# Ternary weights asked for one chunk ahead, a written order for VectorE, and feed-forward's first input between the last unit's projections

## The chip, the cores and the metric

The kernel runs on one core of one Trainium2 chip. A core has a matrix engine (TensorE, PE in the profile; PEld are its weight loads), VectorE (DVE), ScalarE (ACT), GpSimd (POOL) and SyncE (SP), which here only issues DMAs. Each engine carries out its own instructions in the order in which they stand in its queue, and waits on semaphores for the others. The metric is the device time of one execution in microseconds; lower is better.

## What is computed

The input is x, 2 sequences of 1024 rows of 512. Four residual layers follow one another:

```python
x = x + attn_a(layernorm(x))      # gated linear recurrence
x = x + ffn(layernorm(x))         # ternary feed-forward
x = x + attn_b(layernorm(x))      # differential attention
x = x + ffn(layernorm(x))         # the same feed-forward again
```

The change lies in the first layer and in the entry to the second. The first is, with 16 heads of 32:

```python
q, k, v, a, g = split(x @ w_in.T, 5)
q = q * rsqrt(mean(q*q, per head) + eps);  k = tanh(k)
a = clip(sigmoid(a + 2), 0.6, 0.9995);     u = k * v
# per chunk of 64 rows, the state being carried from chunk to chunk
prefix = cumprod(a);  acc = cumsum(u / max(prefix, 1e-6))
mem = prefix * (state + acc)
y = sigmoid(g) * (q * mem) + (1 - sigmoid(g)) * v
return y @ w_out.T
```

The feed-forward takes its weights in ternary form. In groups of 64, `scale = max(mean(|w|), 1e-8)`, and the weight becomes `clip(round(w/scale), -1, 1) * scale`. It computes `silu(x @ gate.T) * (x @ up.T)`, scales it by its root mean square, and multiplies it by the projection.

## The kernel before

All 16 tiles of x (128 rows each) stay in SBUF as `xres`. The first layer, called the gated stage here, works on four blocks t = 0 to 3 of 512 rows. What happens in a block:

- **Input.** `Input(t)` takes the layernorm statistics of the block's four tiles (`layernorm_stats`: two VectorE operations a tile, lines 109 and 110, a square root on ACT, line 112, a reciprocal, line 116). `normal(j)` normalises tile j on VectorE (line 127), and `turn(j)` transposes it on TensorE (line 136) and copies it on ACT (line 265) into `xt`.
- **Queries.** `queries(t, xt)` projects q in four pieces (`pq`), copies and squares each on ACT, and sums the squares by head with matmuls into `pss` (line 280). A square root on ACT and three VectorE operations (lines 300 to 304, among them a reciprocal of 3.3 us) make `rq`, the heads' factors.
- **Units.** For each quarter c of the channels, TensorE makes k and v (`kv`), then a and g (`ag`), each projection with `project` (8 matmul records). Then a small matmul `pr` (line 389) spreads `rq`. ACT makes u = tanh(k), v, a and the gate. VectorE clips a, makes `prefix` with a scan, runs the state's scan `mem`, multiplies it by `qn` and by the gate. GpSimd makes the products u·v and u·prefix, mem − v and the sum `yt`; in the very last unit VectorE does these too (`other`).
- **Output.** The products of `yt` with `w_out` (line 421), tile by tile, are added to `xres` on VectorE (line 426). The next block's queries stand before the output products of a block.

PSUM has two double banks ("big") for `kv` and `ag` and four single ones ("bank") for all else.

Beside this runs the making of ternary weights, in 16 chunks f of 768 KB. `Ternary.__init__` issues three loads on SyncE's queue (line 155), then ACT takes magnitude (line 157) and sign (line 159). `mean(i)` is a matmul `pm` on TensorE (line 166) and a copy on ACT (line 167), three a chunk. `finish` is six VectorE operations (lines 171 to 179). `quantise(i)` does piece i of the chunk at hand: 0 to 2 are means, and 3 is `finish`, the write of the result to DRAM as `w_kept` (line 319), and the next chunk's `Ternary`. The pool that holds the chunks has two buffers of each kind, except `one`. Blocks 0 to 2 each work on four chunks: in the units, one ends at c = 1 and one at c = 3; one has its means in the queries and ends after them; and one has its pieces behind the output products of tiles 0 to 3. In block 3 each of c = 0 to 2 has a chunk of its own. Chunk 0 is done in block 0's queries.

The order of instructions is settled in two ways. Inside `tc.manual_schedule` an engine's instructions keep the order of the program text. Other engines are ordered by a planner, which places what it expects to be ready. In the gated stage, TensorE has the written order (up to the last block's output products), and VectorE has it in the very first input alone.

The feed-forward (`feed_forward`, also for the last layer) begins by asking for all 16 chunks of `w_kept` (line 569). Its first input is `FeedForwardInput(which, 0, ...)`: statistics of x tiles 0 to 3, which are final once block 0's output is added, four normalised tiles, four transposes, and for each a rounded copy `hi` on ACT (line 474) and the difference `lo` on VectorE (line 475). They stand ahead of its first gate projection, `g` (line 524).

Of the kernel before, what the change touches and what calls it, by code (L numbers as in the profile page):

```python
# [10 lines left out]
F32 = mybir.dt.float32  # L11
F32R = mybir.dt.float32r
# [5 lines left out]
P = 128  # L18
D = 512
# [4 lines left out]
BLK = 512  # L24
# [18 lines left out]
def kernel(  # L43
# [95 lines left out]


# [3 lines left out]
    class Ternary:  # L144
# [3 lines left out]
        def __init__(self, pool, f, tiles):  # L148
            self.pool, self.f, self.n = pool, f, f"{f}_{tiles[0]}"
            self.shape = [P, len(tiles), D]  # L150
            self.w = pool.tile(self.shape, F32R, tag="w32", name=f"w32_{self.n}")
            w32 = self.w.bitcast(F32)
            for i, e in enumerate(tiles):
                src = w_pt[ts(f, P), :] if e == 2 else w_gu[e * NF + f].rearrange("p c n -> p (c n)")
                nc.sync.dma_start(out=w32[:, i, :], in_=src)
            self.mag = pool.tile(self.shape, BF, tag="mag", name=f"mag{self.n}")
            nc.scalar.activation(self.mag, w32, AF.Abs)
            self.sign = pool.tile(self.shape, BF, tag="sign", name=f"sign{self.n}")
            nc.scalar.sign(self.sign, w32)
            self.scale = None  # L160

# [20 lines left out]
    with ExitStack() as s:  # L182
# [15 lines left out]
        w_q, w_k, w_v = (load_w_in(i) for i in range(3))  # L198
# [6 lines left out]
        chunk = [Ternary(tp, 0, range(3))]  # L205
        w_a, w_g = (load_w_in(i) for i in (3, 4))
        load_x(TPB, 2 * TPB)
        w_out = wa.tile([P, NKC, D], F32, name="w_out")
# [64 lines left out]
        def queries(t, xt):  # L273

            q = ap_.tile([P, NKC, BLK], F32, tag="q", name=f"q{t}")
# [21 lines left out]
            mean_square(*late.pop())  # L297
            rq = ap_.tile([16, BLK], F32, tag="rq", name=f"rq{t}")
            nc.scalar.activation(rq, pss[:16, :], AF.Sqrt, bias=rms_eps[:16])
            nc.vector.reciprocal(rq, rq)  # L300
            parts = rq_parts[t % 2]
            hi, lo = parts[:16], parts[32:48]
            nc.vector.tensor_copy(hi, rq)
            nc.vector.tensor_sub(lo, rq, hi.bitcast(F32))
            quantise(3)
            return q, parts

        load_x(2 * TPB, NTT)

        def quantise(i):  # L310

            now = chunk[0]
            if now is None:
                return
            if i < 3:
                now.mean(i, bank)
                return
            now.finish(now.w)
            nc.sync.dma_start(out=w_kept[now.f].bitcast(F32), in_=now.w.bitcast(F32))
            chunk[0] = Ternary(tp, now.f + 1, range(3)) if now.f + 1 < NF else None  # L320

        order = ExitStack()
        order.enter_context(tc.manual_schedule(engines={mybir.EngineType.PE}))
        before = [None] * NKC
        first = Input(0, at_once=False)
        with tc.manual_schedule(engines={mybir.EngineType.DVE}):
            for j in range(TPB + 1):
                if j < TPB:
                    first.measure(j)
                if j:  # L330
                    first.normal(j - 1)
                    first.turn(j - 1)
        xt = first.xt
        q, rq = queries(0, xt)
        for t in range(NBLK):
            yt = wa.tile([P, NKC, BLK], F32, tag="yt", name=f"yt{t}")
            following = None
            for c in range(NKC):
                n = f"{t}_{c}"
                kv, ag = big(f"kv{n}"), big(f"ag{n}")  # L340
                project(kv[:, 0, :], w_k, c, xt)
                project(kv[:, 1, :], w_v, c, xt)

                if t < NBLK - 1:
                    pieces = ((2,), (), (3,)) if c % 2 else ((0,), (1,), ())
                else:
                    pieces = ((0, 1), (2,), (3,)) if c < NKC - 1 else ((), (), ())
                for i in pieces[0]:
                    quantise(i)
                project(ag[:, 0, :], w_a, c, xt)  # L350
                project(ag[:, 1, :], w_g, c, xt)
                for i in pieces[1]:
                    quantise(i)
                if following and c > 1:
                    for j in (2 * c - 4, 2 * c - 3):
                        following.turn(j)
# [9 lines left out]
                other = nc.gpsimd if (t, c) < (NBLK - 1, NKC - 1) else nc.vector  # L366
# [12 lines left out]


# [6 lines left out]

                pr = bank(f"pr{n}")
                nc.tensor.matmul(pr, headrow[:, c, :], rq, start=True, stop=True)
                qn = ap_.tile([P, BLK], F32, tag="qn", name=f"qn{n}")  # L390
                nc.vector.tensor_mul(qn, pr, q[:, c, :])
                nc.vector.tensor_mul(mem, mem, qn)
                other.tensor_sub(mem, mem, v)
                nc.vector.tensor_mul(mem, mem, gate)
                other.tensor_add(yt[:, c, :], mem, v)

                if t + 1 == NBLK and c == 0:
                    ff_stats = layernorm_stats(range(TPB), "f0_0")
                if t + 1 < NBLK and c < 2:
                    if c == 0:  # L400
                        following = Input(t + 1)
                    following.normal(0 if c == 0 else 1)
                for i in pieces[2]:
                    quantise(i)
                if following and c == 2:
                    following.normal(2)
                    following.normal(3)

            if following:
                xt = following.xt  # L410
                q_next, rq_next = queries(t + 1, xt)
            products = [(j, k) for j in range(TPB) for k in range(NKC)]
            if not following:

                order.close()
                products.sort(key=lambda jk: jk[1] == NKC - 1)
            po = {}
            for j, k in products:
# [5 lines left out]
                if k == NKC - 1:  # L424
                    xi = xres[t * TPB + j]
                    nc.vector.tensor_add(xi, xi, po[j])
                    if following:
                        quantise(j)
            if following:
                q, rq = q_next, rq_next  # L430

    edge_sb = ctx.enter_context(tc.tile_pool(name="edge", bufs=1, reuse_waits="tile"))
# [20 lines left out]
    class FeedForwardInput:  # L455


        def __init__(self, which, t, pool, tag, stats=None):
            self.n = f"{which}_{t}"
            self.which, self.tiles = which, range(t * TPB, (t + 1) * TPB)  # L460
            self.stats = stats or layernorm_stats(self.tiles, f"f{self.n}")
            self.xs = pool.tile([P, 2, NKC, BLK], F32R, tag=tag, name=f"xs{self.n}", bufs=1)
            self.xn = {}

        def normal(self, j):
            i = self.tiles[j]
            self.xn[j] = normal(i, j, self.stats, f"f{self.which}_{i}")

        def tile(self, j, psum):
            if j not in self.xn:  # L470
                self.normal(j)
            pt = transposed(self.xn.pop(j), f"f{self.which}_{self.tiles[j]}", psum)
            hi, lo = (self.xs[:, e, :, ts(j, P)] for e in range(2))
            nc.scalar.copy(hi, pt)  # L474
            nc.vector.tensor_sub(lo, pt, hi.bitcast(F32))

# [5 lines left out]
    def feed_forward(which, store, first=None, beside=None):  # L482


        with ExitStack() as s:
# [84 lines left out]
            if not first:  # L570
                first = FeedForwardInput(which, 0, edge_sb, "xt", ff_stats)
                for j in range(TPB):
                    first.tile(j, ring)
# [44 lines left out]
        0, False, None,  # L618
# [533 lines left out]
```

## Time and profile before

| | us |
|---|---|
| median of 3 runs | 2145.2 (2144.91 to 2147.58) |
| the profiled execution | 2146.65 |
| its span, first to last instruction | 2144.9 |
| TensorE busy | 2108.8 |
| VectorE busy | 1069.1 |
| ScalarE busy | 835.2 |
| GpSimd busy | 449.8 |

The gated stage and the entry to the feed-forward fill the first 400 us of the span. All rows are of one execution. In a timeline, a row has its start, the time of its group from first start to last end, engine, line, operation, output and inputs and how many instructions are merged; brackets give the idle time of the engine before the row and who ended it. In a list of waits the figures are the total, the number of waits and the longest.

### The profile page before, as it was taken

To read this page: it belongs to the slowest core of one execution; us is meant where nothing else is said; L and a number is where in the kernel's file an instruction comes from. 1 tells how busy PE (TensorE), PEld (TensorE's weight loads), DVE (VectorE), ACT (ScalarE), POOL (GpSimd) and SP (SyncE) were. 2 spreads that over 40 slices of the span, in tenths; PEclk is the share of its full clock that TensorE was granted. 3 is DMA by queue.
4 is the path that set the end of the run, shared out by engine and by line. 5 is a ranking of instruction groups with operands and counts; after the bars stand their busy time and mean duration, and the time that the engine had idled before them with its cause. 6 is when DMAs were issued, how large, how long until landed. Compare 5 with 4: busy or idle time off the path is not lost.

```text
span 2144.9 us, 28054 instructions
## 1 busy us (share of the span) xinstructions
PE 2108.8 (98%) x10615; PEld 1242.2 (58%) x10624; DVE 1069.1 (50%) x2272; ACT 835.2 (39%) x1590; POOL 449.8 (21%) x812
## 2 busy tenths in 40 slices
PE   8999999999999999999999999999999999999998
PEld 3444444688888854444444444444545447888887
DVE  5766686533343234555555465464546662433322
ACT  4444333234344322444444422243434523333333
POOL 1312212122122221111111113021212221121212
PEclk9999999999999999999999999999999999999999
DMA  6111211600000111111110101201110033000000
GB/s 255 59 59 62 86 59 74 250 1 1 1 1 1 35 46 37 41 26 41 23 44 21 46 8 37 57 20 42 24 32 15 14 111 132 20 1 20 1 20 20
DMA packets 50999, 98.71 MB, mean 46 GB/s; under 512 B 10800, under 2 KB 19120, under 8 KB 50864
## 3 DMA queue, kind: packets, MB, share of 16 engines
q1 hardware_dynamic: 50864, 96.93, 13.8%
q8 instruction: 83, 1.36, 0.3%
q14 instruction: 52, 0.43, 0.1%
HBM read 58.75 MB, written 16.78 MB: 35 GB/s over the span
## 4 chain that ended last, share of the span: by engine, by line
PE 83%; DVE 8%; DMA 4%; ACT 2%; issue 1%; POOL 1%; SPq 1%; DVEq 0%; ACTq 0%; POOLq 0%
PE y L904 12%; PE g L524 11%; PE u L524 11%; PE f_out L545 11%; PE s L805 10%; PE pq L737 8%; PE t L866 8%; PE pv L702 3%; PE b_out L965 2%; DMA w<-in_w_pt_dram 1%; DMA w_kept<-w 1%; DVE one L174 1%; PE kv L269 1%; DVE w L179 1%; PE ag L269 1%
## 5 line engine op out<-in xcount | busy, mean ns | idle before, releaser
L882 ACT ACTIVATE pr<-t 128x512 f32<-128x512 f32 (+3 forms) x768 | 314.8, 497 | 380.6 <-PE t L874 380.4
L815 DVE CUSTOM_DVE_ANT_0 s<-s,causal 128x128 f32<-128x128 f32 (+3 forms) x512 | 245.3, 510 | 126.1 <-PE s L805 117.4
L904 PE MATMUL y<-pr,val 128*64 128x512 f32 (+3 forms) x1536 | 291.6, 501 | 0.2 <-POOL pr L885 0.2
L539 POOL TENSOR_TENSOR ssq<-ssq,sq 128x512 f32<-128x512 f32 x120 | 155.9, 1299 | 603.6 <-ACT sq L538 603.6
L530 DVE TENSOR_TENSOR h<-h,u 128x512 f32<-128x512 f32 x128 | 88.0, 688 | 362.0 <-PE u L524 355.9
L524 PE MATMUL g<-xs,w 128*128 128x512 f32 x1024 | 262.4, 398 | 0.9 <-ACT xs L474 0.7
L545 PE MATMUL f_out<-w,hs 128*128 128x512 f32 x1024 | 257.7, 394 | 0.3 <-DVE hs L533 0.3
L820 DVE TENSOR_REDUCE nmax<-s 128x1 f32<-128x512 f32 x256 | 165.0, 686 | 184.4 <-PE s L805 184.3
L524 PE MATMUL u<-xs,w 128*128 128x512 f32 x1024 | 256.4, 392 | 0.0
L805 PE MATMUL s<-gr,gr 32*128 32x512 f32 (+3 forms) x1536 | 248.8, 492 | 2.6 <-DVE nmax L815 2.6
L524 PEld LDWEIGHTS u<-xs,w 128*128 128x128 f32 x1024 | 192.4, 188 | 43.5
L545 PEld LDWEIGHTS f_out<-w,hs 128*128 128x128 f32 x1024 | 191.6, 188 | 43.9 <-DVE hs L533 1.1
L524 PEld LDWEIGHTS g<-xs,w 128*128 128x128 f32 x1024 | 190.9, 189 | 44.0 <-ACT xs L474 0.9
L866 PE MATMUL t<-gr,gr 32*128 32x512 f32 (+3 forms) x1536 | 198.8, 533 | 0.0
L904 PEld LDWEIGHTS y<-pr,val 128*64 128x64 f32 x1536 | 93.5, 136 | 179.9 <-issue 105.7
L737 PE MATMUL pq<-b_xt,w_qk 128*128 128x512 f32 x384 | 176.0, 603 | 0.0
L805 PEld LDWEIGHTS s<-gr,gr 32*128 32x128 f32 x1536 | 147.6, 185 | 46.8 <-issue 14.0
L532 ACT CAST hs<-h 128x512 fp32r<-128x512 f32 x128 | 79.4, 621 | 236.6 <-DVE h L530 236.6
L885 POOL TENSOR_SCALAR_AFFINE_SELECT pr<-pr 128x256 f32<-128x256 f32 x256 | 101.3, 408 | 332.2 <-ACT pr L882 332.2
L529 ACT ACTIVATE h<-g 128x512 f32<-128x512 f32 x128 | 76.5, 598 | 224.3 <-PE g L524 224.1
L533 DVE TENSOR_TENSOR hs<-h,hs 128x512 fp32r<-128x512 f32 x128 | 88.6, 692 | 83.1 <-ACT hs L532 83.1
L737 PEld LDWEIGHTS pq<-b_xt,w_qk 128*128 128x128 f32 x384 | 69.6, 189 | 88.0 <-issue 74.0
(155 smaller groups left out, 2211.0 us busy)
## 6 DMA issues: line engine op xcount, KB each, us to landing
w<-w_kept SPq DMA_DIRECT2D x32, 768.0 KB, 8.7
w_kept<-w SPq DMA_DIRECT2D x16, 768.0 KB, 3.2
gr<-gr SPq DMA_DIRECT2D x96, 128.0 KB, 2.3
w<-in_w_gu_dram SPq DMA_DIRECT2D x32, 256.0 KB, 2.8
share<-ys SPq DMA_DIRECT2D x128, 64.0 KB, 2.0
w_in<-in_w_in_t_dram SPq DMA_DIRECT2D x5, 1024.0 KB, 11.2
x<-in_x_dram SPq DMA_DIRECT2D x16, 256.0 KB, 7.1
w<-in_w_pt_dram SPq DMA_DIRECT2D x16, 256.0 KB, 3.5
```

The source lines that it names most:

```text
L524: nc.tensor.matmul(po, ws[f][:, part, ts(k, P)], xs[:, e, k, :], start=(k == 0 and e == 0), stop=(k == NKC - 1 and e == 1),)
L533: nc.vector.tensor_sub(hp[:, 1, :], h, hp[:, 0, :].bitcast(F32))
L539: nc.gpsimd.tensor_add(ssq, ssq, sq)
L545: nc.tensor.matmul(po[j], hp[:, e, ts(j, P)], ws[f][:, 2, :], start=(f == 0 and e == 0), stop=(f == NF - 1 and e == 1),)
L737: nc.tensor.matmul(po, w[:, k, ts(kind, P)], xts[b][:, k, ts(e, BLK)], start=(k == 0), stop=(k == NKC - 1),)
L805: nc.tensor.matmul(part, queries[:, ts(j, P)], keys[:, first : first + nk], start=True, stop=True,)
L815: nc.vector.tensor_tensor_reduce(part, part, causal[:, BLK - part.shape[-1] :], -1.0, 3.0e38, ALU.add, ALU.min, top,)
L820: nc.vector.tensor_reduce(top, part, AX.X, ALU.max, negate=True)
L866: nc.tensor.matmul(banks[u, e][:, :nq], keys[:, ts(kb, P)], queries[:, (qb + 1) * BLK - nq : (qb + 1) * BLK], start=True, stop=False,)
L882: nc.scalar.activation(pr[:, e, :nq], banks[u, e][:, :nq], AF.Exp)
L885: nc.gpsimd.affine_select(out=pr[:, :, :P], in_=pr[:, :, :P], compare_op=ALU.is_ge, fill=0.0, base=0, pattern=[[0, 2], [1, P]], channel_mu ...
L904: nc.tensor.matmul(y[64 * e : 64 * e + 64, lo:], all_values[:, HV * (NH * kb + h) : HV * (NH * kb + h) + 64], pr[:, e, : BLK - lo], start= ...
```

## The change

1. **Chunks.** `Ternary.__init__` now only issues the loads. ACT's magnitude and sign are in a new method `begin`. Two chunks are in hand: the one worked on and the one already asked for. `finish` of chunk f is followed by `begin` of f + 1 and the loads of f + 2. Chunk 1's loads stand before those of `w_out`; x tiles 8 to 15 are loaded after block 0's queries in the text.
2. **Order.** VectorE has the written order in the whole gated stage, and both engines keep it to the end of the last block's output products. Within a unit, `pr` and `qn` stand ahead of the state's scan. A block's `Input` with its statistics is moved forward: `Input(1)` stands behind block 0's queries, and `Input(t + 2)` at the end of block t. `normal(0)` and `normal(1)` stand in units 0 and 1 behind `qn`; the transposes stand between the k/v and the a/g projections of units 2 and 3, with `normal(2)` and `normal(3)` between those of unit 2.
3. **Queries.** The last `pss` matmul with the square root (`roots`) and the three VectorE operations (`factors`) are moved: in block 0 behind the first k projection, otherwise behind the output products of tile 0, with the chunk's `finish` between them. The next chunk's pieces are spread anew over the output products.
4. **Feed-forward's first input** is made in the last block: statistics and `normal(0)`, `normal(1)` in unit 2 behind the product with `qn`, the four tiles before and after the a projection of unit 3. Its `xs` takes the tile in which `w_q` and `w_k` now lie together. The last block's output products run over k = 0 and 1 of all tiles first, then k = 2, then k = 3.

The core of the diff:

```diff
+        def begin(self):
+            pool, w32 = self.pool, self.w.bitcast(F32)
             self.mag = pool.tile(self.shape, BF, tag="mag", name=f"mag{self.n}")
             nc.scalar.activation(self.mag, w32, AF.Abs)
             self.sign = pool.tile(self.shape, BF, tag="sign", name=f"sign{self.n}")
             nc.scalar.sign(self.sign, w32)
             self.scale = None
+            return self
...
-        w_q, w_k, w_v = (load_w_in(i) for i in range(3))
+        w_qk = edge_sb.tile([P, 2, NKC, D], F32, tag="xt", name="w_in_qk")
+        w_q, w_k = w_qk[:, 0], w_qk[:, 1]
...
-        chunk = [Ternary(tp, 0, range(3))]
+        chunk = [Ternary(tp, 0, range(3)).begin()]
         w_a, w_g = (load_w_in(i) for i in (3, 4))
         load_x(TPB, 2 * TPB)
+        chunk.append(Ternary(tp, 1, range(3)))
...
-            mean_square(*late.pop())
...
-            quantise(3)
-            return q, parts
-
-        load_x(2 * TPB, NTT)
+            def roots():
+                mean_square(*late.pop())
+                nc.scalar.activation(rq, pss[:16, :], AF.Sqrt, bias=rms_eps[:16])
+
+            def factors():
+                nc.vector.reciprocal(rq, rq)
+                hi, lo = parts[:16], parts[32:48]
+                nc.vector.tensor_copy(hi, rq)
+                nc.vector.tensor_sub(lo, rq, hi.bitcast(F32))
+
+            return q, parts, roots, factors
...
-            chunk[0] = Ternary(tp, now.f + 1, range(3)) if now.f + 1 < NF else None
+            chunk[0] = chunk[1].begin() if chunk[1] else None
+            chunk[1] = Ternary(tp, now.f + 2, range(3)) if now.f + 2 < NF else None
...
-        order.enter_context(tc.manual_schedule(engines={mybir.EngineType.PE}))
+        fixed = {mybir.EngineType.PE, mybir.EngineType.DVE}
+        order.enter_context(tc.manual_schedule(engines=fixed))
...
-        q, rq = queries(0, xt)
+        q, rq, roots, factors = queries(0, xt)
+        load_x(2 * TPB, NTT)
+        following = Input(1)
...
+                project(kv[:, 0, :], w_k, c, xt)
+                if t + c == 0:
+                    roots()
+                    factors()
+                project(kv[:, 1, :], w_v, c, xt)
+                if t + c == 0:
+                    quantise(3)
+                if not last and c > 1:
+                    for j in (2 * c - 4, 2 * c - 3):
+                        following.turn(j)
+                        if c == 2:
+                            following.normal(j + 2)
                 for i in pieces[0]:
                     quantise(i)
+                ff_tiles = range(TPB) if last and c == NKC - 1 else ()
+                turn = lambda name: bank(name)
+                for j in ff_tiles[:2]:
+                    ff_first.tile(j, turn)
                 project(ag[:, 0, :], w_a, c, xt)
+                for j in ff_tiles[2:]:
+                    ff_first.tile(j, turn)
                 project(ag[:, 1, :], w_g, c, xt)
...
                 nc.vector.tensor_mul(qn, pr, q[:, c, :])
+                if not last and c < 2:
+                    following.normal(c)
...
                 other.tensor_sub(mem, mem, v)
+                if last and c == NKC - 2:
+                    ff_first = FeedForwardInput(0, 0, edge_sb, "xt")
+                    ff_first.normal(0)
+                    ff_first.normal(1)
                 nc.vector.tensor_mul(mem, mem, gate)
                 other.tensor_add(yt[:, c, :], mem, v)
...
-            if not following:
-                order.close()
-                products.sort(key=lambda jk: jk[1] == NKC - 1)
+            if last:
+                products.sort(key=lambda jk: max(jk[1], 1))
...
-                    if following:
-                        quantise(j)
+                    if not last:
+                        if j == 0:
+                            roots()
+                            quantise(3)
+                            factors()
+                        for i in ((), (0,), (1, 2), (3,))[j]:
+                            quantise(i)
+            if not last:
+                q, rq = q_next, rq_next
+                following = Input(t + 2) if t + 2 < NBLK else None
+        order.close()
...
     feed_forward(
-        0, False, None,
+        0, False, ff_first,
```

## The prediction, made before the changed kernel was run

> **What bounds the kernel now.** First the page: TensorE is busy 98% of the span, so only its pauses can be won, and every new pause costs its full length.
>
> ```profile
> PE 2108.8 (98%) x10615; PEld 1242.2 (58%) x10624; DVE 1069.1 (50%) x2272; ACT 835.2 (39%) x1590; POOL 449.8 (21%) x812
> ```
>
> Then the waits of TensorE in 0 to 404 us, the part that the diff touches. The transposes' 7.5 are nearly all the kernel's start.
>
> ```profile
> PE xnt_a L136 <- DVE xn_a L127: 7.5, 3, 6.8
> PE pm L166 <- ACT mag L157: 4.7, 2, 2.7
> PE pss L280 <- ACT sq L289: 3.4, 5, 2.1
> PE pq L269 <- ACT a_xt L265: 2.6, 4, 0.7
> PE xnt_f L136 <- DVE xn_f L127: 2.3, 2, 1.9
> PE a_out L421 <- POOL yt L395: 1.0, 1, 1.0
> ```
>
> Third, TensorE's timeline, to place them. The bracket is the idle time before a row and who ended it.
>
> ```profile
> 41.93 0.38 PE L166 MATMUL pm<-mag,groupmean 128*128 128x512 bf16 x1 [2.06 <-ACT mag L157]
> 355.06 1.01 PE L166 MATMUL pm<-mag,groupmean 128*128 128x512 bf16 x2 [2.68 <-ACT mag L157]
> 355.87 8.17 PE L269 MATMUL ag<-a_xt,w_in 128*128 128x512 f32 x16
> 363.90 0.58 PE L389 MATMUL pr<-rq_parts,headrow 128*128 128x512 f32 x1
> 371.18 7.03 PE L269 MATMUL ag<-a_xt,w_in 128*128 128x512 f32 x16
> 397.29 0.63 PE L136 MATMUL xnt_f<-ident,xn_f 128*128 128x128 f32 x4 [1.95 <-DVE xn_f L127]
> 399.32 3.34 PE L524 MATMUL g<-xs,w 128*128 128x512 f32 x7 [0.24 <-DVE xs L475]
> ```
>
> The 16 ag matmuls take 8.17 after the pause and 7.03 elsewhere. Fourth, the stage windows (PEclk is the third figure from the right): the clock was 0.83 and 0.57 after the two pauses.
>
> ```profile
> 355.10:363.90 8.80, 8.80 (x19) 3.82 (x19) 6.26 (x7) 3.21 (x5) 4.96 (x3) 0.83 0.15 62
> 399.00:403.00 4.00, 3.76 (x11) 2.91 (x11) 1.68 (x5) 1.14 (x2) 0.00 (x0) 0.57 1.02 418
> ```
>
> Last, SyncE's waits (14 of 16 chunk loads wait for a `w_kept` write), and VectorE's rows of one `finish`, whose operations stretch beside GpSimd.
>
> ```profile
> SPq L155 <- DMA w_kept<-w: 42.0, 14, 4.8
> ```
>
> ```profile
> 58.26 0.55 DVE L171 TENSOR_SCALAR scale<-scale 128x1536 bf16<-128x1536 bf16 x1
> 58.85 2.70 DVE L174 SCALAR_TENSOR_TENSOR one<-scale,mag 128x1536 bf16<-128x1536 bf16 x1
> 61.58 1.91 DVE L176 TENSOR_TENSOR scale<-scale,mag 128x1536 bf16<-128x1536 bf16 x1
> 63.52 0.96 DVE L177 TENSOR_TENSOR scale<-scale,mag 128x1536 bf16<-128x1536 bf16 x1
> 64.52 0.96 DVE L178 TENSOR_TENSOR scale<-scale,one 128x1536 bf16<-128x1536 bf16 x1
> 65.51 1.76 DVE L179 TENSOR_TENSOR w<-scale,sign 128x1536 fp32r<-128x1536 bf16 x1
> ```
>
> **Units of the sum.** T(c) is the end of unit c's ag projections on TensorE. One project is 8 matmuls of 0.43, 3.44 us. VectorE's gated chain can start at T+0.95 (ACT's `a`: 0.2 late, 0.7 long). By the rows from 50.27 to 58.34 it then takes 6.0 to the product with qn, and 8.0 to the product with gate, between two GpSimd hand-overs. A `finish` takes 7.1 alone (206.24 to 213.37), 9.0 beside two GpSimd operations (above), and 8.0 beside one (0.55, 2.70, three of 0.96, 1.76, with gaps). After it the chunk's write, the load that reuses its buffer and ACT's mag take 7.7 + 1.5 = 9.2 before a pm can start (345.85 written, 353.53 mag, 355.06 pm).
>
> **Asking a chunk ahead.** The buffers stay two. In the trace chunk 1's load was already issued at 28.27, before chunk 0's write at 44.04, and each later one follows the write of the chunk two before it. So chunks 2 to 15 gain nothing: the same wait binds. Only chunk 1 moves, ahead of w_out and eight x tiles (3 MB, some 7 us at the 408 GB/s of those slices), so its mag comes before the pm at 41.93: −2.06. The last pss of block 0 goes behind a k projection: −0.32. Sum −2.4 (bounds 0 and −3). w_out and x come 2 us later, with tens of us of cover.
>
> **Changes of block.** Before, three of them cost 0.63+0.32, 0.64+2.07+0.34 and 0.63+0.68+0.32 = 5.6. The transposes, moved between the k/v and a/g projections, and the last pss, moved behind the first output products, take away these waits. What is late next: VectorE in program order does chunk B's `finish` behind the gated chain of c = 3, not at 182 to 192 around T = 185.4. So it ends at T+0.95+8.0+8.0 = 17.0, and chunk D's first pm can start at 26.2. TensorE reaches it at T + pr 0.4 + queries 17.1 + j0 3.4 + pss 0.9 + j1 3.4 = 25.2: a pause of 1.0. Then `finish` C (7.1) and the factors (3.33+0.40+0.68) stand before the addition of j = 1, so two of four banks stay full and the bank of j = 3 waits for ACT's scale copy: 0.45. Three times 1.45 is 4.35: −1.3 (bounds −5.6 if neither wait comes, +4 if ACT, strictly in order, holds copies behind a mag). The next block's stats (3.3) and two normals lie in VectorE's free time in c = 0 and 2; the square roots have 25 us of cover.
>
> **Chunk 15's pause.** In block 3 each c has a `finish`. Chunk 13's ended 15.5 after T(0) = 330.3, its operations woven into the chain. In order it comes behind it: 0.95+8.0+9.0 = 18.0 (yt and the next u·v run on GpSimd then), so chunk 15's pm can start at T(0)+27.2, where its k/v projections end at 21.9. A pause of 5.3 in place of 2.85: +2.45 (bounds −1 and +7). The clock: the row shows 0.83 over 8.8 us after a pause of 2.85, 1.5 lost. [...]
>
> **Feed-forward's first input.** VectorE, from T(2): chain to the product with qn 6.95; four stats 3.3, 10.25; ACT's root and the reciprocal 0.7, 10.95; normal 0 11.5; normal 1 12.0; gate 12.65; `finish` 15, 8.0 beside yt, 20.65; two lo subtractions 1.3, 21.95; normal 2 22.5. TensorE ends c = 3's k/v projections at 7.3 and now waits there: idle to 11.55, tiles 0 and 1, a-projection to about 17.8 (1.7 of slow clock in it), idle to 22.5, tile 2 to 23.2; hi copy 0.65, lo 0.7, normal 3 0.55: idle to 25.2; tile 3 to 25.9; g-projection 3.44, with 1.7 of slow clock as at 399 (4.0 × 0.43), to 31.0 = T(3). Before, the scheduler had floated these stats to 123 and 218 us and let the rest run behind the products. Then pr 0.4 and products 13.8: feed-forward starts at 45.2. Before: 402.48 − 1.87 = 400.6 at full speed, 36.75 after T(2) = 363.87. So +8.45. This already contains the gains: the yt pause (1.0), the four transpose and xs waits (3.2) and the slow g (1.7) are gone. Bounds +5 and +11: ends of `finish` at 7.1 and 9.0, slow clock of 0 and 3.4. The last yt is ready at T(3)+9.9, its products start at 10.75; weights have 14 us from T(3): no cost.
>
> **Edits costed at nothing.** w_q and w_k share one tile, which later holds the input's xs: its last reader, unit 3's k projection, is done at T(2)+3.9, ahead of the first hi copy at about 12. If the first projection waited for both loads, x, w_q and w_k (3.1 MB) have landed by about 11 us at the rates of the DMA row, and TensorE starts at 12.38. The output products' new order (k = 0, 1 of all j first) needs all four banks at T(3)+5.6; the last qn frees pr's at T(3)+4.8. Without that 0.8 of cover the fourth would pause by as much as qn is late. Later kept-writes on SyncE are followed by chunk loads alone, and at the end by feed-forward's weights, which wait for T(3) anyway.
>
> **Sum:** −2.4 −1.3 +2.45 +8.45 = +7.2. The profiled execution took 2146.65 (span 2144.9 and 1.75 around it), 1.45 above the median; it would become 2153.9, and the median 2145.2 becomes 2152.4.
>
> **Rivals.** (1) Faster: the input's tiles come in time. Its point is whether normals 0 and 1 are ready at T(2)+7.3 and normals 2 and 3 about 4.5 later. Then T(2) to feed-forward is TensorE work alone, 0.4+13.8+2.1+0.4+13.8 = 30.4, −6.3, and the sum −2.4−1.3+2.45−6.3 = −7.6: 2137.6. For it: VectorE is only 50% busy, and another order of these twelve instructions would do it. Against: as the diff reads, stats follow the chain of c = 2 and normal 2 follows `finish` 15; that needs 4 and 11 us less. (2) Even: GpSimd stays out of `finish`'s way, 7.1 each. Then D's pm is just in time (−4.3), chunk 15 waits 3.4 (+0.5), the tail is +7.5: −2.4−4.3+0.5+7.5 = +1.3, 2146.5. For it are 206.24 and 221.19; against, every `finish` that met a yt. (3) Worse: ACT holds unit 0's `a` behind chunk 14's mag, as at 330.48 (a at 333.75). With that chunk's write 2 us later, the chain of block 3 slips 4.8 more, and chunk 15's pause with it: 2157.2. (4) The change does nothing in its first part: in the sum already.
>
> **How the numbers follow.** Forecast 0.60, rival 3 0.12, rival 2 0.17, rival 1 0.11. 0.2% is 4.3 us, about what a measurement of this kernel can tell from no change. Slower 0.72, within it 0.17, faster 0.11. The forecast's own range is 2147 to 2158. The range 2142 to 2160 takes in rivals 2 and 3 and leaves out rival 1 and the far ends.
>
> **What would show it.** Right: no pause at 41.9 and none of ACT's a_xt before pq; a pause of 4 to 6 before chunk 15's pm; two idle stretches of 4 to 5 us at xnt_f released by xn_f inside the last unit; a clock below 0.9 in them; feed-forward starting some 7 us later than 400.6. Wrong: xnt_f without waits, or stats of x0 to x3 on VectorE before T(2).

## The result, and the profile after

| | before | after |
|---|---|---|
| median, us (range, runs) | 2149.18 (2144.91 to 2152.82, 6) | 2161.48 (2158.80 to 2163.92, 6) |
| profiled execution, us (span) | 2146.65 (2144.9) | 2159.2 (2157.4) |
| T(2), the end of unit 2's ag projections in block 3, to feed-forward at full speed, us | 36.7 | 47.9 |

The change made the kernel slower: the ratio is 1.0058 with a 95% interval of 1.0042 to 1.0075. That is 12.3 us by the medians and 12.5 by the spans, where +7.2 was forecast. The direction was right; two terms of the sum were mis-sized, and one of them had the wrong sign. The time itself, 2161.48, lies 9.1 above the 2152.4 of the forecast: 5.1 of that is the change, and 4.0 is the level of before, whose six runs have a median of 2149.18, while the three told of above, which are among the six, had 2145.2.

The share of busy time on the page tells nothing: still 98%, of a longer span.

```profile
PE 2112.4 (98%) x10624; PEld 1245.4 (58%) x10624; DVE 1079.2 (50%) x2272; ACT 831.1 (39%) x1587; POOL 448.8 (21%) x812
```

TensorE's waits from 0 to 420 us do. Columns: total, number, longest. The waits of before at pss, at yt and at feed-forward's g are gone; those at pm and xnt_f rose from 4.7 and 2.3.

```profile
PE xnt_f L136 <- DVE xn_f L127: 12.4, 3, 6.4
PE pm L194 <- ACT mag L184: 10.4, 4, 4.7
PE xnt_a L136 <- DVE xn_a L127: 7.5, 3, 6.8
PE a_out L472 <- ACT scale L195: 1.4, 3, 0.5
PE pq L305 <- ACT a_xt L301: 0.7, 1, 0.7
```

TensorE's timeline places them: one pause at each change of block (here the first and third in full), one before chunk 15's means, three in the last unit.

```profile
117.42 0.38 PE L194 MATMUL pm<-mag,groupmean 128*128 128x512 bf16 x1 [1.95 <-ACT mag L184]
117.63 3.59 PE L472 MATMUL a_out<-w_out,yt 128*128 128x512 f32 x8
...
211.06 0.38 PE L194 MATMUL pm<-mag,groupmean 128*128 128x512 bf16 x1 [1.66 <-ACT mag L184]
...
305.06 0.38 PE L194 MATMUL pm<-mag,groupmean 128*128 128x512 bf16 x1 [2.03 <-ACT mag L184]
305.28 5.29 PE L472 MATMUL a_out<-w_out,yt 128*128 128x512 f32 x8
...
355.99 0.59 PE L194 MATMUL pm<-mag,groupmean 128*128 128x512 bf16 x2 [4.74 <-ACT mag L184]
356.42 8.72 PE L305 MATMUL ag<-a_xt,w_in 128*128 128x512 f32 x16
365.01 0.58 PE L437 MATMUL pr<-rq_parts,headrow 128*128 128x512 f32 x1
378.86 1.97 PE L136 MATMUL xnt_f<-ident,xn_f 128*128 128x128 f32 x8 [6.40 <-DVE xn_f L127]
380.62 5.27 PE L305 MATMUL ag<-a_xt,w_in 128*128 128x512 f32 x8
390.01 0.66 PE L136 MATMUL xnt_f<-ident,xn_f 128*128 128x128 f32 x4 [4.13 <-DVE xn_f L127]
392.53 1.11 PE L136 MATMUL xnt_f<-ident,xn_f 128*128 128x128 f32 x4 [1.86 <-DVE xn_f L127]
393.44 5.68 PE L305 MATMUL ag<-a_xt,w_in 128*128 128x512 f32 x8
```

Here a pause could cost more than its length. The same eight matmuls take 3.59 after one pause and 5.29 after another, and the granted clock in the stage windows (third figure from the right) differs with them: 1.00 after the pause at 211, 0.71, 0.80 and 0.64 after those at 305, 356 and 379.

```profile
211.00:217.00 6.00, 5.48 (x14) 2.39 (x14) 5.73 (x5) 4.88 (x7) 0.00 (x0) 1.00 0.31 131
305.10:311.00 5.90, 5.90 (x11) 2.27 (x10) 5.30 (x4) 3.91 (x5) 0.00 (x0) 0.71 0.36 142
356.40:365.00 8.60, 8.60 (x18) 3.54 (x17) 7.47 (x5) 2.84 (x5) 2.35 (x2) 0.80 0.03 13
378.80:386.00 7.20, 7.03 (x16) 3.69 (x16) 7.13 (x9) 1.17 (x2) 1.51 (x1) 0.64 0.00 0
```

By landmarks of TensorE's timeline, before against after, the 12.5 add up. The first pr comes at 45.71 instead of 49.04: −3.3. From there to block 3's first k projection it takes 269.29 instead of 267.09: +2.2. Block 3 from its first pr to unit 2's pr: 35.82 instead of 33.58, +2.2. From there to feed-forward at full speed (412.9 and 400.6): +11.2. The rest differs by 0.2. So almost nothing behind this point has moved, and two things need an explanation: the changes of block, which were to win 1.3, and the tail, which was to lose 8.45.

### The profile page after: what moved, and what is told of

It is laid out like the page before. It is cut to its first block, busy times and chain, and to the rows that moved or that the text cites. A ratio compares the mean times of both kernels' runs of the same rounds, so it can differ in the third digit from the quotient of the medians.

```text
span 2157.4 us, 28051 instructions
## 1 busy us (share of the span) xinstructions
PE 2112.4 (98%) x10624; PEld 1245.4 (58%) x10624; DVE 1079.2 (50%) x2272; ACT 831.1 (39%) x1587; POOL 448.8 (21%) x812
## 3 DMA queue, kind: packets, MB, share of 16 engines
q1 hardware_dynamic: 50864, 96.93, 13.8%
## 4 chain that ended last, share of the span: by engine, by line
PE 89%; DVE 5%; DMA 3%; ACT 2%; issue 1%; SPq 1%; POOL 0%; DVEq 0%; ACTq 0%; POOLq 0%
PE y L934 12%; PE g L558 11%; PE u L558 11%; PE f_out L579 11%; PE s L835 10%; PE pq L767 8%; PE t L896 8%; PE ag L305 4%; PE kv L305 4%; PE pv L732 3%; PE b_out L995 2%; PE a_out L472 2%; PE pq L305 1%; DMA w<-in_w_pt_dram 1%; DMA w_kept<-w 1%; DVE one L202 1%
```

## The experiments

The last column but one is the time from unit 2's pr in block 3 to feed-forward at full speed (the second group of eight feed-forward matmuls less 1.87, or the third less 3.74 where the second was still slow). In e5, e10 and e11 no mean stands between the projections and pr, and pr is recorded some 0.4 before the projections' end; in the other runs it follows that end. The kernel's first transposes wait 6.8 us in every run; this wait is left out of the last column.

| run | edit | median, us | ratio to before (95%) | unit 2's pr at | to feed-forward | longest pauses |
|---|---|---|---|---|---|---|
| e1 | before, chunk asked ahead only | 2146.56 | 0.9997 (0.9989 to 1.0005) | 363.16 | 37.2 | pm 3.12 |
| e2 | after, VectorE's order left to the planner | 2143.88 | 0.9981 (0.9975 to 0.9988) | 355.02 | 42.4 | xnt_f 4.95, 4.65 |
| e3 | after, input's statistics early | 2154.91 | 1.0034 (1.0021 to 1.0048) | 366.27 | 41.8 | xnt_f 6.14 |
| e4 | after, finish 15 behind the four tiles | 2161.08 | 1.0063 (1.0049 to 1.0076) | 365.97 | 46.6 | xnt_f 6.39 |
| e5 | after, finishes ahead of the chains | 2150.31 | 1.0012 (1.0005 to 1.0019) | 356.04 | 49.3 | xnt_f 14.50 |
| e6 | after, first input as before | 2150.50 | 1.0012 (1.0005 to 1.0019) | 366.23 | 37.2 | pm 5.25 |
| e7 | after, VectorE written in feed-forward too | 2208.02 | 1.0277 (1.0263 to 1.0291) | 366.43 | 44.7 | pm 4.64, xnt_f 4.45 |
| e8 | e2, tiles 2 and 3 among the output products | 2138.01 | 0.9953 (0.9941 to 0.9966) | 354.69 | 36.0 | a_out 3.83 |
| e9 | e2, all four tiles among the products | 2143.50 | 0.9980 (0.9971 to 0.9989) | 354.02 | 42.6 | ff 6.80 |
| e10 | e3 and e5, all four tiles among the products | 2147.97 | 1.0002 (0.9993 to 1.0010) | 361.27 | 40.6 | xnt_a 4.96 |
| e11 | e5 and e6 | 2142.84 | 0.9973 (0.9963 to 0.9983) | 356.14 | 39.5 | a_out 2.69 |

The theory: VectorE's written order is where the time goes, because of what stands ahead of what in it. Its rivals: asking ahead does more (or less) than it seems, ACT is the engine that holds the chunks up, or a written order costs whatever its places.

**e1, one part alone.** Only `begin` and the request ahead are put into the kernel before, with chunk 1's loads ahead of those of `w_out`.

```diff
+        chunk.append(Ternary(tp, 1, range(3)))
...
-            chunk[0] = Ternary(tp, now.f + 1, range(3)) if now.f + 1 < NF else None
+            chunk[0] = chunk[1].begin() if chunk[1] else None
+            chunk[1] = Ternary(tp, now.f + 2, range(3)) if now.f + 2 < NF else None
```

> The kernel before with the first part of the change alone: loads split from begin, two chunks in hand, chunk 1's loads ahead of w_out. Theory A (the two buffers bind, asking ahead gives nothing to chunks 2 to 15): only the pm pause of 2.06 at 41.9 goes, the pauses near 205 and 355 (ACT mag, 2.68) stay; 2 to 3 us less than before. Rival B (loads asked for early were what was missing): the pause near 355 goes as well, with its slow clock, and the time falls by 6 us or more.

The pause at 41.9 is gone, the one before chunk 15's means stays and is longer (3.12 at 354.14, before 2.68), a new one of 0.87 comes at pss (the one of 2.07 is still there, with 2.16), and the time can't be told from before. So of the 2 to 3 us that were expected nothing is seen for certain. In after, which asks ahead in the same way with the same two buffers, 14 chunk loads still wait for a `w_kept` write, 40.0 us in all, where before's 14 wait 42.0.

**e2, the order given back.**

```diff
-        fixed = {mybir.EngineType.PE, mybir.EngineType.DVE}
+        fixed = {mybir.EngineType.PE}
...
-        for j in range(TPB + 1):
+        with tc.manual_schedule(engines={mybir.EngineType.DVE}):
+          for j in range(TPB + 1):
```

The last lines keep the written order for the very first input, as before.

> The changed kernel with VectorE's order given back to the planner (the very first input excepted); all else as changed. Theory A (the order of VectorE's text is what costs: each finish behind its gated chain, the input's stats behind unit 2's chain): the three D pauses (1.7 to 2.0) and chunk 15's 4.74 fall to 3 or less, the two long xnt_f pauses (6.40, 4.13) fall together below 4, and the time is 10 to 16 us below the changed kernel, at or below before. Rival B (the first input has no room between the last unit's projections, whatever the order): the xnt_f pauses still sum to 8 or more and the kernel stays at least 5 us slower than before.

All four pauses at pm are gone, and the kernel is faster than before. By the two ratios the edit is worth 0.77%, some 16 us. In the tail half of the expectation missed: tiles 0 and 1 of the first input are no longer waited for, but tiles 2 and 3 are, with 4.95 and 4.65 where less than 4 in all had been expected, and the tail is 42.4, still 5.7 above before. So VectorE's order is the cause of the pauses at pm, and of a part of what the tail lost. VectorE's timeline of e2 shows what the planner does at the first change of block: `finish` goes first, the gated chain of c = 3 behind it (in after the chain starts at 91.55 and `finish` at 100.05).

```profile
90.81 1.63 DVE L199 TENSOR_SCALAR scale<-scale 128x1536 bf16<-128x1536 bf16 x1
...
97.24 1.76 DVE L207 TENSOR_TENSOR w<-scale,sign 128x1536 fp32r<-128x1536 bf16 x1
98.91 0.42 DVE L425 TENSOR_SCALAR a<-a 128x512 f32<-128x512 f32 x1
```

**e5, the same place by hand.** The order stays written, but each `finish` stands ahead of its unit's chain. In block 3 all three means come behind the v projection with it.

```diff
-                    pieces = ((2,), (), (3,)) if c % 2 else ((0,), (1,), ())
+                    pieces = ((2,), (), ()) if c % 2 else ((0,), (1,), ())
...
-                    pieces = ((0, 1), (2,), (3,)) if c < NKC - 1 else ((), (), ())
+                    pieces = ((0, 1, 2, 3), (), ()) if c < NKC - 1 else ((), (), ())
...
+                if not last and c % 2:
+                    quantise(3)
```

> The kernel after, with only one thing moved: each chunk's finish in blocks 0 to 3 is written in VectorE's order right behind the last of its three means, ahead of the unit's gated chain (after had it behind the chain; in block 3 the three means are given together behind the v projection). Theory A (the place of finish in VectorE's order makes the write, the load and mag late, and so the pauses at pm): the pauses at pm of after (1.95, 1.66, 2.03 at the changes of block and 4.74 before unit 3 of block 3) fall below 0.5 each, the slow clock behind two of them goes, about 10 us are won there. The tail is not helped: the chain of unit 2 now starts behind finish 15, so the first pause at xnt_f is as long or up to 6 longer, the second shorter. In all 2150 to 2157, ratio to the kernel before 1.001 to 1.004. Rival B (ACT, which does the mags in a written order between its gates, holds the chunks up wherever finish stands): the pm pauses stay over 1 each and the time is within 3 us of after's 2161.

No pm waits any more, and unit 2's pr comes at 356.04 instead of 365.01; the price there is one wait of 2.10 for a normal of block 1. So ACT's own order was not what held the chunks up. What is late next is the tail, and by more than expected (the first pause is 8.1 longer, not up to 6): chain 2 and the normals now stand behind `finish` 15.

```profile
378.21 1.97 PE L136 MATMUL xnt_f<-ident,xn_f 128*128 128x128 f32 x8 [14.50 <-DVE xn_f L127]
```

**e3, e4 and e7, inside the tail.** e3 calls the first input's statistics in unit 0 of block 2; e4 moves `finish` 15 behind the input's four tiles; e7 keeps VectorE's written order in feed-forward too, so that nothing of feed-forward can be placed among the input's operations.

```diff
# e3
+                if (t, c) == (2, 0):
+                    ff_stats = layernorm_stats(range(TPB), "f0_0")
...
-                    ff_first = FeedForwardInput(0, 0, edge_sb, "xt")
+                    ff_first = FeedForwardInput(0, 0, edge_sb, "xt", ff_stats)
# e4
+                if ff_tiles:
+                    quantise(3)
...
-                for i in pieces[2]:
+                for i in pieces[2] if (t, c) != (NBLK - 1, NKC - 2) else ():
# e7
-                tc.manual_schedule(engines={mybir.EngineType.PE, mybir.EngineType.Activation})
+                tc.manual_schedule(engines={mybir.EngineType.PE, mybir.EngineType.Activation, mybir.EngineType.DVE})
```

> The changed kernel with the first feed-forward input's statistics moved from unit 2 of block 3 to unit 0 of block 2. Theory A: the first xnt_f pause falls from 6.4 to below 1; finish 15 then starts some 6 us earlier, but it still stands ahead of normal 2, so the second pause grows from 4.1 to about 6; feed-forward starts 6 to 7 us earlier. Rival B (no room in the unit): the input still waits 8 us or more in all and the gain is under 3.

> The changed kernel with chunk 15's finish moved behind the four tiles of the first input in unit 3. Theory A: the first pause stays at 6.4, the second (4.1) goes, the third (1.9) stays; the last gated chain then runs later, behind finish 15, so that the last yt may be waited for by some 3 us; feed-forward starts 2 to 5.5 us earlier than in the changed kernel. Rival B: the pauses move but their sum stays, no gain.

> The kernel after, with VectorE's order kept as written in the feed-forward stage too, so that statistics of later feed-forward blocks can no longer be placed among the first input's operations. Feed-forward itself changes with that and may win or lose by some us elsewhere, so the reading is the trace from 364 to 415 us. Theory A (foreign statistics, about ten operations of 0.2 to 0.6 us, made the first pause at xnt_f 6.4 where 4.2 was forecast): the first pause falls to 4.0 to 4.7. Rival B (the chain of unit 2 itself is longer than forecast): it stays at 6 or more.

e3 takes the first pause (0.75 is left) and 6.1 us of the tail; its second pause is 6.14, as `finish` 15 still stands there. e4 takes the second pause and wins nothing: the last chain runs behind `finish` 15, and the output products wait 3.89 for its qn. Its expectation of a gain missed. e7 answers why the first pause was 6.40. In after, VectorE goes on from the input's four statistics (line 109) to those of later tiles, which belong to later blocks of feed-forward: five such statistics and three of their aggregates (line 110), in the rows from 374.23 to 377.69, stand ahead of the first normals.

```profile
371.82 0.69 DVE L109 BATCH_NORM_STATS2 st_f<-x 128x6 f32<-128x512 f32 x1
...
374.23 1.25 DVE L109 BATCH_NORM_STATS2 st_f<-x 128x6 f32<-128x512 f32 x2
375.40 0.30 DVE L110 BATCH_NORM_AGGREGATE mv_f<-st_f 128x2 f32<-128x6 f32 x2
375.62 1.27 DVE L109 BATCH_NORM_STATS2 st_f<-x 128x6 f32<-128x512 f32 x2
...
377.61 0.16 DVE L116 RECIPROCAL rstd_f<-rstd_f 128x4 f32<-128x4 f32 x1
377.69 0.66 DVE L109 BATCH_NORM_STATS2 st_f<-x 128x6 f32<-128x512 f32 x1
378.27 0.99 DVE L127 TENSOR_SCALAR xn_f<-x,mv_f,rstd_f 128x512 f32<-128x512 f32 x2
```

In e7 the last of the four is followed by the aggregate, the wait for ACT's root, the reciprocal and the normals:

```profile
375.65 0.66 DVE L109 BATCH_NORM_STATS2 st_f<-x 128x6 f32<-128x512 f32 x1
376.34 0.18 DVE L110 BATCH_NORM_AGGREGATE mv_f<-st_f 128x2 f32<-128x6 f32 x1
376.89 0.18 DVE L116 RECIPROCAL rstd_f<-rstd_f 128x4 f32<-128x4 f32 x1 [0.36 <-ACT rstd_f L112]
377.10 1.00 DVE L127 TENSOR_SCALAR xn_f<-x,mv_f,rstd_f 128x512 f32<-128x512 f32 x2
```

The pause falls to 3.83 (4.0 to 4.7 had been expected), and the tail to 44.7 (45.2 in the prediction). The whole of e7 is slower for another reason: in feed-forward, xnt_b then waits 30.6 us for its normals.

**e6, the other half undone.** The first input is made behind the output products again.

```diff
-                for j in ff_tiles[:2]:
-                    ff_first.tile(j, turn)
...
-                for j in ff_tiles[2:]:
-                    ff_first.tile(j, turn)
...
-                    ff_first = FeedForwardInput(0, 0, edge_sb, "xt")
-                    ff_first.normal(0)
-                    ff_first.normal(1)
...
+            if not first:
+                first = FeedForwardInput(which, 0, edge_sb, "xt")
+                for j in range(TPB):
+                    first.tile(j, ring)
```

> The kernel after, with feed-forward's first input made as in the kernel before: behind the output products, its four tiles one after the other. All else of the change stays, VectorE's written order in the gated stage too. Theory A (the tail is where 11 of the 12.3 us went): from unit 2's a/g projections to the first feed-forward product it takes about 37 to 41 us in place of 47.95, so 2150 to 2155; what is left over the kernel before is the pauses at pm (about +2 at the changes of block, +2.2 before unit 3 of block 3, -3.3 at the start, so +1 and what the statistics cost behind the products). Rival B (any use of VectorE's written order loses as much, since the statistics then follow the last addition): feed-forward starts as late as in after, 2159 to 2163.

The tail is back at 37.2, 10.7 less than in after, and the ratio falls from 1.0058 to 1.0012, which is some 10 of the 12.3 us. The pauses at pm stay (10.7 in all).

```profile
366.23 0.58 PE L433 MATMUL pr<-rq_parts,headrow 128*128 128x512 f32 x1
...
405.30 2.09 PE L550 MATMUL u<-xs,w 128*128 128x512 f32 x8
```

**e11, both places mended, the order still written.** It joins the edits of e5 and e6.

> Two of the earlier edits together: every finish ahead of its unit's gated chain, and feed-forward's first input made as in the kernel before, behind the output products. VectorE's order is written throughout the gated stage, as in after. The two remove the two places in the written order that the runs blame. Theory A (a written order costs nothing by itself, its places do): no pause at pm; unit 2's projections of block 3 end at about 356, as in the run with the finishes ahead, and feed-forward starts about 37 to 41 later, at 393 to 397, the first input still waiting a little for the last chain: 2137 to 2142, ratio 0.995 to 0.998. Rival B (the written order stalls VectorE somewhere whatever the places, and the tail takes the backlog): 2146 or more.

Faster than before: with VectorE's order still written and these two things changed, 1.0058 becomes 0.9973. The ratio lies within the expected 0.995 to 0.998, the median just above the expected 2137 to 2142. So a written order need not lose; its places did. A little of rival B is seen: two short waits for normals of the next block (2.10 and 1.04, in the xnt_a line, whose other 7.5 are the kernel's start) and one of 2.69 for qn, behind `finish` 15 and the chain of unit 2. No run has the planner's order together with the first input as before, so what a written order costs at best is not shown.

```profile
PE xnt_a L136 <- DVE xn_a L127: 10.6, 5, 6.8
PE a_out L466 <- DVE qn L437: 2.7, 1, 2.7
```

**e8, e9 and e10, towards a better version.** e8 is e2 with tiles 2 and 3 moved from between the last unit's a and g projections to behind the eighth output product.

```diff
-                for j in ff_tiles[2:]:
-                    ff_first.tile(j, turn)
...
+                if last and at == 8:
+                    for i in (2, 3):
+                        ff_first.tile(i, lambda name: big(name)[:, 0, :])
```

> The kernel after, with VectorE's order left to the planner in the gated stage (as in the run that came out at 0.998), and with tiles 2 and 3 of feed-forward's first input moved from between the a and g projections of the last unit to behind the eighth output product. Theory A (the two pauses of about 4.8 at xnt_f are what is left; tiles 2 and 3 have no need to be done so early): the pause of tiles 2 and 3 goes, tiles 0 and 1 keep one of up to 5, the last yt may be waited for by up to 4: 2135 to 2141, ratio 0.994 to 0.997. Rival B (the planner puts the normals of tiles 2 and 3 late wherever they are called, or the last yt is waited for by as much as was won): 2142 to 2146, ratio 0.998 to 1.000.

Both pauses of e2 at xnt_f are gone, and e8 beats both kernels: 0.9953. So in e2 it was the place of tiles 2 and 3 in TensorE's order that cost. One pause is left, for an output bank that a tile of the input held until its subtraction:

```profile
375.66 7.02 PE L474 MATMUL a_out<-w_out,yt 128*128 128x512 f32 x12 [3.83 <-DVE xs L162]
```

e9 was to take that one away with tiles 0 and 1 behind the eighth product and 2 and 3 behind the fourteenth, the pair in one buffer. e10 has the same placing in a written order, with the edits of e5 and e3.

> The kernel after, with VectorE's order left to the planner in the gated stage, as in the run at 0.998, and with all four tiles of feed-forward's first input taken out of the last unit: tiles 0 and 1 stand behind the eighth of the 16 output products, tiles 2 and 3 behind the fourteenth, in the PSUM buffers of k/v and a/g. Theory A (the pause of 3.83 that was left with tiles 0 and 1 in the unit came from an output bank held by tile 1 until its subtraction): no pause over 1 in the last unit, the last yt or normals 2 and 3 waited for by up to 3; 2133 to 2138, ratio 0.993 to 0.996. Rival B (the planner puts the normals and subtractions ahead of the last chain anyhow, and the last yt comes as much later): 2138 to 2142.

> The same placing of the four tiles, but with VectorE's written order kept throughout the gated stage as in after, and with the places changed that the runs so far blame: every finish ahead of its unit's gated chain (as in the run with the finishes ahead) and the input's statistics in unit 0 of block 2. Theory A (it was the places in the written order that cost, not a written order as such): no pause at pm over 0.5, no pause of TensorE in the last unit's projections, 1 to 4 in the output products for the last yt or for normals 2 and 3; feed-forward starts 32 to 35 us after unit 2's projections; 2131 to 2138, ratio 0.992 to 0.996. Rival B (a written order makes VectorE wait for its slowest input where the planner's would do something else, and loses some us whatever the places): 2141 or more.

Both missed. The second tile of a pair waited for the first one's subtraction. In e9 the planner had put that behind the last chain (6.80, the other pair 1.40); in e10 it followed at once (1.40 twice). e10 waited 3.09 for the last qn besides, and got a pause of 4.96 in block 2, where the early statistics and a `finish` stand ahead of the next block's second normal; in e11, without the early statistics, the same pause is 1.04. By its time alone e10 lies where its rival B was expected (2141 or more). As other places in its order were bad, it does not tell the theories apart; e11 does.

## Why the prediction was right, and where it was wrong

Slower was right. Two steps failed: the pause before chunk D's means at the changes of block, whose term was 1.0 and measured 1.66 to 2.03, with a slow clock (0.71) behind the third that had been put at nothing; and the time at which the first normals are ready in the tail, T(2)+11.5 in the prediction and some T(2)+13.8 in the trace.

**Asking a chunk ahead: right.** −2.4 forecast, −3.3 measured. The pause of 2.06 is gone. Some 0.7 of the rest lies in the first 16 pq matmuls (8.60 instead of 9.32), which took 8.60 to 10.06 in the runs, whatever the edit, at a granted clock given as 1.00 in before and in after; it is not the change's, and its cause is open. Chunks 2 to 15 gained nothing, as e1 shows.

**Changes of block: the step that had the wrong sign, −1.3 forecast and +2.2 measured.** Its two waits came where it put them, and the bank's 0.45 was exact (0.46 three times). The term that was too small is D's pause: 1.0 forecast, 1.95, 1.66 and 2.03 measured, 2.6 more in all. What failed is "T+0.95+8.0+8.0 = 17.0", its start and the length of the chain. ACT's rows at the third change, where the last 16 projections start at 271.10 and end at T = 278.0 (16 × 0.43 later), show `a` behind the mag and sign of a chunk that had just landed, and behind the copies that these had held up:

```profile
273.65 1.48 ACT L184 ACTIVATE mag<-w 128x1536 bf16<-128x1536 f32 x1 [9.10 <-DMA w<-in_w_pt_dram]
275.04 1.47 ACT L186 ACTIVATE sign<-w 128x1536 bf16<-128x1536 f32 x1
276.41 1.05 ACT L301 COPY a_xt<-xnt_a 128x512 f32<-128x512 f32 x2
...
278.78 0.73 ACT L418 ACTIVATE a<-ag,two 128x512 f32<-128x512 f32 x1
```

VectorE's chain and `finish` follow:

```profile
279.55 1.00 DVE L424 TENSOR_SCALAR a<-a 128x512 f32<-128x512 f32 x1 [5.04 <-ACT a L418]
...
288.05 0.55 DVE L199 TENSOR_SCALAR scale<-scale 128x1536 bf16<-128x1536 bf16 x1
...
294.35 1.76 DVE L207 TENSOR_TENSOR w<-scale,sign 128x1536 fp32r<-128x1536 bf16 x1
```

`a` began 0.8 after T there, 0.4 and 0.7 after T at the first two changes, where 0.2 had been put. So the chain began at T+1.6, T+1.2 and T+1.4. It then took 8.4 to 8.5 before `finish` could start, instead of 8.0 (its first operation, the clip of a, took 1.00 here and at the first change, 0.42 in the row of e2 above), and `finish` took 8.1. So `finish` ended at T+18.1 at the third change and T+17.7 and T+17.8 at the first two, where 17.0 was forecast, and D's pm could start at T+27.1, T+27.0 and T+26.7 instead of T+26.2; TensorE was there at T+25.1, as forecast within 0.1. The late start and the longer chain have about equal shares in this. That ACT, strictly in order, might hold copies behind a mag stood in the prediction as the bound of +4 on this term, and was counted at nothing; the measured term lies within that bound. To this the third pause added 1.7 of slow clock (5.29 for 3.60, at 0.71), which had been counted at none. Those are 4.3; other small gains take the stretch to 3.5 above the forecast. That the order of `finish` is the cause of the pauses is shown by e2 and e5; ACT's share in their size was read from the trace and not tried alone.

**Chunk 15's pause: right.** +2.45 forecast, +2.2 measured: a pause of 4.74 instead of 2.68, and 16 ag matmuls in 8.72 instead of 8.17. `finish` 13 ended at T(0)+17.9, where 18.0 had been worked out. Both pauses had slow clock behind them: 0.83 over 8.8 us in before, 0.80 over 8.6 us in after. The forecast's 2.45 holds no difference in clock; the 16 matmuls took 0.55 more.

**Feed-forward's first input: right in kind, +8.45 forecast, +11.2 measured.** The three idle stretches came in the order given: 4.25, 4.7 and 2.0 forecast, 6.40, 4.13 and 1.86 measured. The term that failed is "four stats 3.3, 10.25; ACT's root and the reciprocal 0.7, 10.95; normal 0 11.5": it took a written order to be closed. Up to the product with qn VectorE was where it was forecast (T(2)+6.9 for 6.95). Then the statistics of later blocks, which are emitted where VectorE has no written order, went in between, and TensorE could go on at T(2)+13.9 instead of 11.55. What came behind the longer pause was also slower: the first eight transposes took 1.97 and the a-projection 5.27 (at a granted clock of 0.64), behind e7's pause of 3.83 they took 1.48 and 4.97. In e7, without the foreign statistics, the tail is 44.7, within 0.5 of the forecast's 45.2.

**The rivals.** Rival 1 needed the normals in time and said that another order would do it. e3 (the first pause) and e8 (all of them, but with TensorE's order changed as well) show that the normals can be in time, though the 30.4 us of bare TensorE work are not reached: 36.0 in e8. Rival 2, `finish` at 7.1, did not come: at the changes of block `finish` took 8.1 (100.05 to 108.11). Rival 3 did not come in block 3: there unit 0's `a` ran at 329.37, ahead of the mag at 330.90.

**The sum.** The misses are −0.9 at the start, +3.5 at the changes of block, −0.2 at chunk 15 and +2.75 in the tail: +5.1, from 7.2 to 12.3. That the first two have opposite signs hides a little of the second.

## What to carry to other kernels

When an engine's order is written out, walk along it as a queue and ask of each long job what stands behind it: an 8 us `finish` behind an 8 us chain delayed a write, a load and a mag, and TensorE paid for it; moved ahead, it cost a wait of 2.1 there and one of 14.5 in the tail, until the tail's first tiles were moved as well. Ask too whether the order is closed: work emitted elsewhere without an order can still be put into it. And price a step that sits on ACT with what ACT has to do first, above all with a wait for a DMA that stands ahead of short copies (9.10 at the third change of block).

## What the runs showed of the hardware

In these runs the length of a pause did not by itself decide whether TensorE came back slow. After 1.66 and 1.95 us the granted clock was 1.00 (211 to 217 and 117 to 123), after 2.03 it was 0.71; before's 2.68 was followed by 0.83, and e11's 2.69, in the output products, by 1.00. The third change of block shows it at one place in the program: e6's pause of some 2.2 (its four pauses at pm are 10.7 in all, the other three 1.84, 1.39 and 5.25) was followed by a clock of 0.72, e3's longer one of 2.62 by eight matmuls in 3.59, as in after at 1.00. The rows are of e11, e6 and e3:

```profile
378.70:387.00 8.30, 8.27 (x20) 3.72 (x21) 5.70 (x9) 0.00 (x0) 0.00 (x0) 1.00 0.88 343
305.30:311.50 6.20, 5.94 (x11) 2.30 (x10) 5.83 (x4) 4.19 (x6) 0.00 (x0) 0.72 0.32 129
308.10 0.38 PE L194 MATMUL pm<-mag,groupmean 128*128 128x512 bf16 x1 [2.62 <-ACT mag L184]
308.32 3.59 PE L474 MATMUL a_out<-w_out,yt 128*128 128x512 f32 x8
```

Where it came back slow, the price was of one size for two very different pauses: 1.7 behind 2.03 (5.29 for 3.60) and 1.7 behind 4.74 (8.72 for 7.03); with the two pm in front, which took 1.01 for 0.59, it was 2.1 behind e6's 5.25 (8.73 for 7.03). What decides between 1.95 and 2.03, or between e6's 2.2 and e3's 2.62, these runs leave open.
